# Reordering VectorE's work inside each phase of a fused state-space mixer, and moving three accumulator merges from GpSimd to VectorE

## The chip, the cores and the metric

The kernel runs on one core of one Trainium2 chip. The metric is the device time of one execution in microseconds (us); the time given for a kernel is the median of its runs. The five engines of the core are written as the profile writes them: PE (TensorE, matrix products), DVE (VectorE), ACT (ScalarE), POOL (GpSimd), SP (the queue that issues nearly all DMAs). PEld is PE's loading of weights, which runs beside its products.

## The reference

The input is 2 sequences of 512 tokens with 512 features, so 1024 tokens in 8 tiles of 128. Four residual blocks follow each other: a block-sparse linear layer, a quantised feed-forward block, a state-space mixer, and the feed-forward block again. The change touches only the mixer:

```python
proj = hidden_states @ in_proj_w.T               # gate | x, B, C | dt
xc = conv_general_dilated(xc, conv_w, ...) + conv_b   # causal, 4 taps, per channel
hBC = silu(transpose(xc))                        # x: 128 heads x 64; B, C: 8 groups x 128
dt = softplus(dt + dt_bias);  A = -exp(A_log)
Gm = einsum('bclhn,bcshn->bclsh', Cch, Bch)      # chunks of 128 tokens
M = Gm * exp(segment_sum(A * dt))                # decayed scores
Y_diag = einsum('bclsh,bcshp->bclhp', M, x * dt)
states = einsum('bclhn,bclhp->bchpn', B_decay, x * dt)   # carried from chunk to chunk
Y_off = einsum('bclhn,bchpn->bclhp', Cch, states) * state_decay
y = Y_diag + Y_off + D * x
y = y * rsqrt(mean(y**2) + eps) * norm_w * silu(gate)
return y @ out_proj_w.T
```

## The kernel before

**Phases.** The 8192 channels of x are 64 tiles of 128. A phase (`ph` 1 to 31) takes two of them, for both sequences: four *units*, `(0,0), (0,1), (1,0), (1,1)`. A phase overlaps three generations of work. For its own two tiles it computes the x projection (`x_front`), the convolution and the gate projection (`g_front`). For the tiles of the phase before it does the recurrence: transposed tokens (`tokens`), chunk states (`both_states`), decayed scores (`half_scores`, `back_scores`), the scan (`half_scan`) and the gating. For the tiles two phases back it does the output projection (`o()`, from `out_seven`). Phases 2 to 30 (`mid` in the code) have one written order of these steps. Phases 3, 7, 11, 15, 19, 23 and 27 also start the next group's B and C (`new_group`), and the phases 4, 8, ..., 28 after them compute that group's products of B and C (`group_scores`). Phase 31 is `final`: it does the output projection by plain products (`outs`).

**Order.** PE, ACT and DVE run in exactly the order in which the program is written (`manual_schedule`). POOL and SP are ordered by the scheduler. An instruction that waits holds up everything behind it on its engine.

**Seven-product blocks.** `seven` multiplies a 2x2 block matrix by Strassen's scheme in seven products over three PSUM banks x, y, z; `out_seven` does the same for two halves of the output projection, 14 products in a phase. In `seven` the third write of bank y may start only when DVE has read the second out of it: the product `s3*t3` (PE line 185) waits for the sum on line 206, the product `a22*t4` for that on line 211. In `out_seven` (PE line 1020, DVE sums on line 1034) the product 14 waits for DVE's sum of product 12, which reads the same bank.

**Deferred lists.** Two kinds of DVE work are kept in lists and issued when the program calls for them. `flush()` issues the waiting score products `m = m * gm` (line 900), which make the operands of the scan's products (line 919). `drain(3)` issues three convolution taps (line 734) of one 128x512 tile. `skipped` (line 939) takes the scan's result out of PSUM; `gated[k]()` (line 942) multiplies it with norm weight and gate. After that ACT squares y (line 948) and POOL adds the square to `sq_acc` (line 949).

**States.** `both_states(k)` multiplies into a PSUM bank (line 848). The first chunk's state is then copied, by ACT (line 857) where `by_act` is true and by DVE (line 859) otherwise, and the later chunks are formed by DVE, four instructions a unit (line 862).

**Merge.** In the output projection one product belongs to all four quarters of the accumulator `acc`. It is summed in a tile of its own, `common[0]`, and at the end of phase 30 `merge()` (line 1058) adds it to the other three quarters, with three 128x1024 additions on POOL.

Of the kernel before, what the change touches and what calls it, by code (L numbers as in the profile page):

```python
# [37 lines left out]
def kernel(  # L38
# [25 lines left out]
    nc = tc.nc  # L64
# [604 lines left out]
    def mixer(waiting, step_args, loaded):  # L669

        with ExitStack() as st:
# [18 lines left out]
            acc = x_sb  # L690
# [50 lines left out]
            def drain(n=None):  # L741

                n = len(taps) if n is None else min(n, len(taps))
                for f in taps[:n]:
                    f()
                del taps[:n]

            def silu(dst, src):
                nc.scalar.activation(dst, src, AF.Silu)  # L749

            def run(steps):
                for _ in steps:
                    pass
# [30 lines left out]
            n_ph = NCT // PP  # L784
# [26 lines left out]
            def g_front(left, gts, tags="proj"):  # L811

                for j, b in units:
                    gts[j, b] = act.tile([P, SEQ], F32, tag=f"gt{j}{b}", name="gt")
                later = []
                steps = seven(
                    left, tags, lambda j, b: gts[j, b], lambda j, b, ps: later.append((gts[j, b], ps)), False
                )
                return steps, later

            def x_tokens(ct, b, xc):

                h0 = 2 * ct
                cs = slice(b * NCH, (b + 1) * NCH)
                px = psum.tile([P, NCH, 2, HD], F32, tag="tr", name="x_tr")
                for c in range(NCH):
                    nc.tensor.transpose(  # L827
                        px[:, c].rearrange("p h d -> p (h d)"), xc[:, c * P : (c + 1) * P], ident
                    )
                x_dt = wrk.tile([P, NCH, 2, HD], F32, name="x_dt", bufs=4)  # L830
                nc.vector.tensor_tensor(
                    x_dt, px, dt[:, cs, h0 : h0 + 2].unsqueeze(3).to_broadcast([P, NCH, 2, HD]), ALU.mult
                )
                x_dec = wrk.tile([P, NCH - 1, 2, HD], F32, name="x_dec", bufs=2)
                nc.gpsimd.tensor_tensor(
                    x_dec,
                    x_dt[:, : NCH - 1],
                    dec[:, b, :, h0 : h0 + 2].unsqueeze(3).to_broadcast([P, NCH - 1, 2, HD]),
                    ALU.mult,
                )  # L840
                return x_dt, x_dec

            def states(ct, b, x_dec, b_tok, by_act):

                h0 = 2 * ct
                pst = psum.tile([P, NCH - 1, 2, HD], F32, tag="tr", name="pst")
                for c in range(NCH - 1):
                    nc.tensor.matmul(  # L848
                        pst[:, c].rearrange("p h d -> p (h d)"),
                        lhsT=b_tok[:, c, :],  # L850
                        rhs=x_dec[:, c].rearrange("p h d -> p (h d)"),
                        start=True,
                        stop=True,
                    )
                state = wrk.tile([P, NCH - 1, 2, HD], F32, name="state", bufs=4)
                if by_act:
                    nc.scalar.copy(state[:, 0], pst[:, 0])  # L857
                else:
                    nc.vector.tensor_copy(state[:, 0], pst[:, 0])
                for c in range(1, NCH - 1):  # L860
                    for hh in range(2):
                        nc.vector.scalar_tensor_tensor(  # L862
                            state[:, c, hh, :],
                            state[:, c - 1, hh, :],
                            e_last[:, b, c - 1, h0 + hh : h0 + hh + 1],
                            pst[:, c, hh, :],
                            ALU.mult,
                            ALU.add,
                        )
                return state  # L870
# [7 lines left out]
            def flush():  # L878
                for f in mults:
                    f()  # L880
                mults.clear()
# [65 lines left out]
            def squares(b, y):  # L947
                nc.scalar.activation(y, y, AF.Square)  # L948
                nc.gpsimd.tensor_add(sq_acc[:, b, :], sq_acc[:, b, :], y)  # L949

            def out_project(ph, ts, gts, wo, tag="yo", adds=None):
# [27 lines left out]
            common = []  # L979
            quarter = [  # L980
                (slice(b * NCH, (b + 1) * NCH), slice(n * DH, (n + 1) * DH)) for b in range(2) for n in range(2)
            ]
# [69 lines left out]
                        )  # L1052
                return steps

            def merge():

                for rows, cols in quarter[1:]:
                    nc.gpsimd.tensor_add(acc[:, rows, cols], acc[:, rows, cols], common[0])

            xcs, gts = {}, {}  # L1060
            groups = {}
# [2 lines left out]
            def half_scores(k, c, heads, later=None):  # L1064

                j, b = units[k // 2]
                if k % 2 == 0:
                    heads[j, b] = []
                    heads["bc"] = load_sums(c + j, b)
                heads[j, b].append(scores(c + j, b, k % 2, heads["bc"], later))  # L1070
# [44 lines left out]
            gate, later = g_front(wg, gts)  # L1115
# [40 lines left out]
            for ph in range(1, n_ph + 1):  # L1156
                front, last = ph < n_ph, ph >= 2
# [18 lines left out]
                def all_squares():  # L1176
                    for b, y in ys:
                        squares(b, y)
                    ys.clear()

                def tokens(k):
                    j, b = units[k]
                    xts[j, b] = x_tokens(c1 + j, b, xcs[j, b])

                def both_states(k, by_act=False):
                    for j, b in units[2 * k : 2 * k + 2]:
                        sts[j, b] = states(c1 + j, b, xts[j, b][1], groups[c1 // CTG][b][1], by_act)

                def back_scores(k):
                    half_scores(k, c1, heads)  # L1190
# [25 lines left out]
                if mid:  # L1216
                    outs7 = out_seven(lefts, rights, ph == 2)

                    def o():
                        product, summed = outs7.pop(0)  # L1220
                        product()
                        summed()

                    next(steps)
                    tokens(2)
                    tokens(3)
                    o()
                    next(steps)
                    back_scores(2)
                    o()  # L1230
                    o()
                    next(steps)
                    both_states(0, True)
                    back_scores(3)
                    o()
                    next(steps)
                    o()
                    flush()
                    next(steps)
                    drain(3)  # L1240
                    o()
# [9 lines left out]
                    gated = [f for _, f in scans]  # L1251
# [2 lines left out]
                    flush()  # L1254
                    back_scores(5)
                    o()
                    gated[0]()
                    o()
                    o()
                    flush()  # L1260
                    back_scores(6)
                    if made:
                        group_scores(made, groups[c0 // CTG], [0])
                    o()
                    gated[1]()
                    flush()
                    back_scores(7)
                    if made:
                        group_scores(made, groups[c0 // CTG], [1])
                    o()  # L1270
                    all_squares()
                    made = None
                    if ph == n_ph - 2:
                        merge()
                    if new_group:

                        flush()
                        steps, made = group((c0 + PP) // CTG, wbc, "yo")
                        for i, _ in enumerate(steps):
                            if i in (0, 1, 3, 5):  # L1280
                                drain(3)
                        gate, later = g_front(wg, gts_new)
                    else:
                        gate, later = g_front(wg, gts_new, ("proj", "yo", "yo"))
                        next(gate)
                        flush()
                    wx = load_pair(NCT + c0 + PP, NCT + c0 + PP + 1)
                    wo = load_out(ph - 1)
                    finish(half_scan(units[2:], "tr"))
# [11 lines left out]
                    for u in units:  # L1301
                        silu(xcs_new[u], xcs_new[u])
                    flush()
                    run(gate)
                else:
                    next(steps)
                    if not last:
                        group_scores(made, groups[0], [0])
                    else:
                        flush()  # L1310
                    next(steps)
                    if not last:
                        group_scores(made, groups[0], [1])
# [3 lines left out]
                        back_scores(2)  # L1317
                    tokens(2)
                    tokens(3)
                    next(steps)  # L1320
                    if last:
                        back_scores(3)
                    next(steps)
                    flush()
# [12 lines left out]
                    if not last:  # L1337
                        drain()
                        both_states(1)
                        gate, later = g_front(wg, gts_new)  # L1340
# [31 lines left out]
                    else:  # L1372
                        gate, later = g_front(wg, gts_new)
# [252 lines left out]
```

## Time and profile before

| | |
|---|---|
| median of 3 runs | 2304.89 us (2302.44 to 2306.73) |
| the profiled execution: its own time, its span | 2304.02 us, 2302.3 us |
| PE busy | 2242.4 us, 97% |
| DVE busy | 1805.7 us, 78% |
| POOL busy | 1243.9 us, 54% |
| ACT busy | 1180.2 us, 51% |
| mean granted PE clock | 0.998 |

The time is told by the span plus some 1.7 us around it (2304.02 less 2302.3). A busy PE is not a PE at its peak, so the 97% says only that PE is seldom without an instruction, not that the products are cheap. The stages stand in the timeline as follows: block-sparse layer and first feed-forward block up to about 330 us, mixer up to about 2035 us, second feed-forward block to the end. Within the mixer a phase of the plain kind is 49.2 us long (for instance from 622.73 to 671.96 us), one with a new group 62.4 us (671.96 to 734.32), the one after it 51.3 us (734.32 to 785.59).

### The profile page before, as it was taken

Reading aid. Unit: us, or ns where it says so; the run is one execution under the profiler, and the core shown is the slowest. Engines: PE = TensorE matmul, PEld = TensorE weight load, DVE = VectorE, ACT = ScalarE, POOL = GpSimd, SP = SyncE. Lnnn points to the kernel's source line nnn. Section 1 sums busy time; section 2 is a strip of 40 time slices with the busy share of each in tenths; the row PEclk is TensorE's granted clock in tenths of the full one; section 3 lists DMA queues with packets and bytes.
Section 4 is the critical chain, followed back from the end, with each engine's and each line's share of the span. In section 5 each row is a group of like instructions: output and inputs, shape, how many; then the busy total and the mean of one; then the engine's idle time right before and its main releaser. Section 6 shows DMA issues by size and latency. Waiting matters only on the chain.

```text
span 2302.3 us, 30183 instructions
## 1 busy us (share of the span) xinstructions
PE 2242.4 (97%) x10704; PEld 1411.4 (61%) x10704; DVE 1805.7 (78%) x3042; ACT 1180.2 (51%) x2532; POOL 1243.9 (54%) x1206
## 2 busy tenths in 40 slices
PE   9999999999999999999999999999999999999999
PEld 5445865656665666666566656666666665544468
DVE  5456568888888888888888888888888888865553
ACT  4111056756666665666566656656655666631100
POOL 3765024656655666566556555664665665527620
PEclk9999999999999999999999999999999999999999
DMA  5563021222222222222221222221222322326600
GB/s 188 191 199 105 28 74 55 74 74 65 73 74 65 74 85 71 74 74 74 64 74 65 77 68 75 74 83 58 81 75 63 110 65 74 119 83 223 201 24 28
DMA packets 145783, 201.59 MB, mean 88 GB/s; under 512 B 7136, under 2 KB 92000, under 8 KB 145632
## 3 DMA queue, kind: packets, MB, share of 16 engines
q1 hardware_dynamic: 145056, 198.61, 27.1%
q8 instruction: 85, 1.39, 0.3%
q10 hardware_dynamic: 576, 1.05, 0.1%
q14 instruction: 66, 0.54, 0.1%
HBM read 194.91 MB, written 4.72 MB: 87 GB/s over the span
## 4 chain that ended last, share of the span: by engine, by line
PE 83%; DVE 14%; issue 2%; ACT 1%; DMA 1%; POOL 0%; ACTq 0%; SPq 0%; POOLq 0%; DVEq 0%
PE proj L185 29%; PE yo L185 17%; PE po L1020 10%; PE ffn_o L556 7%; DVE m L900 5%; DVE x_sb L1034 5%; PE py L919 4%; PE pst L848 4%; PE py L928 3%; PE x_tr L827 2%; PE po L956 2%; DVE gt L942 1%; PE pg L486 1%; PE pu L486 1%; DVE xc L734 1%
## 5 line engine op out<-in xcount | busy, mean ns | idle before, releaser
L906 POOL TENSOR_TENSOR ce<-ce,c_t 128x384 f32<-128x384 f32 x256 | 267.7, 1051 | 340.7 <-ACT ce L902 335.0
L185 PE MATMUL proj<-xn_t,w 128*128 128x512 f32 x824 | 384.6, 593 | 2.0 <-DVE gt L206 1.7
L892 ACT ACTIVATE m<-bc,acs 128x128 f32<-128x128 f32 x1024 | 324.9, 390 | 4.4 <-PE py L919 4.4
L185 PEld LDWEIGHTS proj<-xn_t,w 128*128 128x128 f32 x824 | 153.0, 190 | 146.4 <-issue 137.7
L1034 DVE TENSOR_TENSOR x_sb<-x_sb,po 128x512 f32<-128x512 f32 x340 | 228.9, 679 | 9.5 <-PE po L1020 4.9
L171 POOL TENSOR_TENSOR ws<-w 128x256 f32<-128x256 f32 x96 | 72.9, 760 | 292.2 <-DMA w<-in_win_t_dram 242.1
L734 DVE SCALAR_TENSOR_TENSOR xc<-proj,cw,xc 128x511 f32<-128x511 f32 (+2 forms) x288 | 214.6, 746 | 6.6
L900 DVE TENSOR_TENSOR m<-m,gm 128x512 f32<-128x512 f32 x256 | 218.6, 876 | 0.0
L919 PE MATMUL py<-m,x_dt 128*64 128x128 f32 x2048 | 194.1, 278 | 13.7 <-DVE m L900 13.6
L949 POOL TENSOR_TENSOR sq_acc<-sq_acc,y 128x512 f32<-128x512 f32 x128 | 178.4, 1400 | 46.5 <-ACT y L948 43.8
L185 PE MATMUL proj<-tq,ws 128*128 128x512 f32 x432 | 199.2, 592 | 0.0
L1020 PE MATMUL po<-wo,gt 128*128 128x256 f32 x696 | 177.0, 384 | 0.0
L919 PEld LDWEIGHTS py<-m,x_dt 128*64 128x64 f32 x2048 | 135.8, 137 | 49.0 <-issue 25.8
L899 ACT ACTIVATE m<-m 128x512 f32<-128x512 f32 x256 | 161.3, 630 | 7.4
L185 PE MATMUL yo<-xn_t,w 128*128 128x512 f32 x328 | 151.7, 595 | 12.8 <-DVE tmp L206 12.8
L928 PE MATMUL py<-ce,state 128*64 128x128 f32 x1536 | 157.6, 274 | 0.0
L862 DVE SCALAR_TENSOR_TENSOR state<-state,e_last,pst 128x64 f32<-128x64 f32 x512 | 107.0, 276 | 60.2 <-ACT state L857 57.7
L185 PE MATMUL yo<-tq,ws 128*128 128x512 f32 x336 | 153.4, 599 | 0.2 <-ACT acs L714 0.2
L1020 PEld LDWEIGHTS po<-wo,gt 128*128 128x128 f32 x696 | 125.5, 190 | 30.9 <-issue 7.1
L749 ACT ACTIVATE xc<-xc 128x512 f32<-128x512 f32 x128 | 72.5, 621 | 134.3 <-DVE xc L734 133.9
L731 ACT ACTIVATE xc<-proj,cb,cw 128x512 f32<-128x512 f32 x96 | 74.4, 778 | 129.5 <-DVE proj L225 76.6
L942 DVE SCALAR_TENSOR_TENSOR gt<-y,nw,gt 128x512 f32<-128x512 f32 x128 | 137.1, 1071 | 2.5
(228 smaller groups left out, 4559.5 us busy)
## 6 DMA issues: line engine op xcount, KB each, us to landing
bc<-acs_d SPq DMA_DIRECT2D x128, 512.0 KB, 3.8
w<-in_win_t_dram SPq DMA_DIRECT2D x64, 512.0 KB, 3.8
wo<-in_wo_t_dram SPq DMA_DIRECT2D x31, 512.0 KB, 5.0
wi<-in_down_w_dram SPq DMA_DIRECT2D x14, 512.0 KB, 4.0
zi<-in_down_z_dram SPq DMA_DIRECT2D x14, 512.0 KB, 4.8
sf<-in_down_s_dram SPq DMA_DIRECT2D x14, 512.0 KB, 4.2
wi<-in_gate_w_dram SPq DMA_DIRECT2D x13, 512.0 KB, 4.3
zi<-in_gate_z_dram SPq DMA_DIRECT2D x13, 512.0 KB, 5.2
```

The costliest lines, as they stand in the source:

```text
L185: nc.tensor.matmul(ps, lhsT=a[:, kc, :], rhs=b[:, kc, :], start=(start and kc == 0), stop=(stop and kc == KH - 1), skip_group_check=True,)
L556: nc.tensor.matmul(ps, lhsT=a[:, k, :], rhs=b(k), start=(start and k == 0), stop=(stop and k == KF - 1), skip_group_check=True,)
L734: nc.vector.scalar_tensor_tensor(dst[:, s:], ps[:, : SEQ - s], cw[:, t, 3 - s : 4 - s], dst[:, s:], ALU.mult, ALU.add)
L892: nc.scalar.activation(m[:, c, :], bc[:, hh, c * P : (c + 1) * P], AF.Relu, bias=acs[:, t, h : h + 1], scale=-1.0,)
L899: nc.scalar.activation(m, m, AF.Exp, scale=-1.0)
L900: mults.append(lambda: nc.vector.tensor_mul(m, m, shared[b][2]))
L906: nc.gpsimd.tensor_mul(ce, ce, c_t[:, P:].rearrange("p (c l) -> p c l", l=P))
L919: nc.tensor.matmul(py[hh * HD : (hh + 1) * HD, c * P : (c + 1) * P], lhsT=x_dt[:, c, hh, :], rhs=m[:, c, :], start=True, stop=(c == 0),)
L928: nc.tensor.matmul(py[hh * HD : (hh + 1) * HD, c * P : (c + 1) * P], lhsT=state[:, c - 1, hh, :], rhs=ce[:, c - 1, :], start=False, stop=True,
L949: nc.gpsimd.tensor_add(sq_acc[:, b, :], sq_acc[:, b, :], y)
L1020: nc.tensor.matmul(banks[k][:, c, :], lhsT=a[:, t], rhs=b, start=(start and c == 0), stop=stop, skip_group_check=True,)
L1034: nc.vector.tensor_add(q, q, banks[k])
```

## The change

It has five parts.

1. In phases 2 to 30 the score products of the second pair (`back_scores(2)` and `(3)`) are issued on DVE before the states of the first pair rather than three steps after them; ACT works out `back_scores(3)` before, not after, `both_states(0)`. A `flush()` is added at the head of the phase; the list is empty there except in phase 2.
2. `both_states(0)` no longer has ACT copy the first states: two ACT copies a phase become two DVE copies.
3. The gatings: `gated[0]` is issued two output sums later, `gated[1]` after all eight score products and after the output sums.
4. With a new group, each pair of taps left over from x moves one step later, behind the sums of B's and C's products; the last three taps move to the end of the gate projection.
5. The three merges leave POOL at the end of phase 30 and are issued on DVE in phase 31, at three places.

```diff
-            def merge():
-                for rows, cols in quarter[1:]:
-                    nc.gpsimd.tensor_add(acc[:, rows, cols], acc[:, rows, cols], common[0])
+            def merge(k):
+                rows, cols = quarter[k]
+                nc.vector.tensor_add(acc[:, rows, cols], acc[:, rows, cols], common[0])
...
                     tokens(2)
                     tokens(3)
+                    flush()
                     o()
                     next(steps)
                     back_scores(2)
                     o()
                     o()
+                    back_scores(3)
                     next(steps)
-                    both_states(0, True)
-                    back_scores(3)
+                    flush()
+                    both_states(0)
                     o()
                     next(steps)
                     o()
-                    flush()
                     next(steps)
                     drain(3)
...
                     back_scores(5)
                     o()
-                    gated[0]()
                     o()
                     o()
+                    gated[0]()
                     flush()
                     back_scores(6)
...
                     o()
-                    gated[1]()
                     flush()
                     back_scores(7)
...
                     o()
+                    flush()
+                    gated[1]()
                     all_squares()
                     made = None
-                    if ph == n_ph - 2:
-                        merge()
                     if new_group:
-                        flush()
                         steps, made = group((c0 + PP) // CTG, wbc, "yo")
                         for i, _ in enumerate(steps):
-                            if i in (0, 1, 3, 5):
+                            if i in (1, 3, 5):
                                 drain(3)
                         gate, later = g_front(wg, gts_new)
                     else:
                         gate, later = g_front(wg, gts_new, ("proj", "yo", "yo"))
                         next(gate)
-                        flush()
...
                     flush()
+                    next(gate)
+                    drain(3)
                     run(gate)
                 else:
                     next(steps)
                     if not last:
                         group_scores(made, groups[0], [0])
                     else:
-                        flush()
+                        merge(1)
...
                     tokens(2)
                     tokens(3)
+                    if last:
+                        merge(2)
                     next(steps)
                     if last:
+                        merge(3)
                         back_scores(3)
```

PE's own order is the same before and after. On ACT only the two copies a phase go and `back_scores(3)` moves ahead of where they were. POOL's scheduled order follows: the third score's `ce` product (line 906) now stands ahead of the third and fourth `x_dec` (line 835), and the weight sums of the output projection (lines 988 to 990) stand between the two additions to `sq_acc` instead of behind both. SP's order is unchanged.

## The prediction

> **What bounds the kernel now.** I read the page first, then PE's waits over phases 2 to 30, then the timeline of a plain phase (616.7 to 666 us), a new-group phase and phases 2, 30 and 31, engine by engine.
>
> ```profile
> PE 2242.4 (97%) x10704; PEld 1411.4 (61%) x10704; DVE 1805.7 (78%) x3042; ACT 1180.2 (51%) x2532; POOL 1243.9 (54%) x1206
> PE 83%; DVE 14%; issue 2%; ACT 1%; DMA 1%; POOL 0%; ACTq 0%; SPq 0%; POOLq 0%; DVEq 0%
> ```
>
> PE bounds it: it is without an instruction for 60 us of 2302. The change leaves PE's instructions and their order alone, so all that can be won is time in which PE waits (and slow clock after it). PE's waits between 440 and 1940 us:
>
> ```profile
> PE py L919 <- DVE m L900: 13.6, 21, 2.3
> PE po L1020 <- DVE x_sb L1034: 12.9, 21, 0.6
> PE yo L185 <- DVE tmp L206: 12.8, 7, 1.8
> PE pgm L778 <- DVE gm L779: 1.9, 7, 0.3
> ```
>
> All are for DVE: 41.2 us, the ceiling apart from clock. One of each in the timeline:
>
> ```profile
> 648.37 1.13 PE L1020 MATMUL po<-ws,gt 128*128 128x256 f32 x4 [0.62 <-DVE x_sb L1034]
> ...
> 653.67 0.54 PE L919 MATMUL py<-m,x_dt 128*64 128x128 f32 x5 [0.56 <-DVE m L900]
> ...
> 705.72 3.70 PE L185 MATMUL yo<-xn_t,w 128*128 128x512 f32 x8 [1.83 <-DVE tmp L206]
> ```
>
> And what DVE does in a plain phase:
>
> ```profile
> 627.18 1.62 DVE L862 SCALAR_TENSOR_TENSOR state<-state,e_last,pst 128x64 f32<-128x64 f32 x8 [1.99 <-ACT state L857]
> ...
> 632.06 1.29 DVE L900 TENSOR_TENSOR m<-m,gm 128x512 f32<-128x512 f32 x2
> ...
> 652.17 1.45 DVE L900 TENSOR_TENSOR m<-m,gm 128x512 f32<-128x512 f32 x1
> ```
>
> DVE waits at the head of a phase (0.95, 1.10, 0.17, 1.99 and 0.73 us up to 630 us), then works almost without a gap until the next phase's transposes. It is late only in the second half. The change moves work into the gap at the head and lets the sums and score products for which PE waits go ahead of gatings, which PE needs only in the next phase.
>
> **The change, part by part (plain phase, 13 of them: 5, 6, 9, 10, ... 29).** *Score products and states.* ACT ends the exponential of the third score at 623.6; without the state copies (0.27 each, behind a wait of 2.88 for PE) it goes straight on with the fourth: four biases 1.28 and an exponential 0.63, ready at 625.9. DVE, free at 625.2, issues both products at 625.2 and 625.9: 1.3 us uncovered by POOL, up to 2.75 beside it (the row at 1952.44 of phase 31), so done by 626.6 to 627.9. Then two copies (0.28) and eight state steps (1.62): done by 629 to 630.1, where before it was 628.8. Behind them stands the sum on line 211, due for PE's `a22*t4` at 633.4: it ends at 631.0. So the added wait on ACT's exponential costs nothing; its cover is these 2.4 us. On POOL, the two later `x_dec` move behind one more `ce` (1.0 us): they end near 629.4, and their product starts at 637.7.
> The taps at 633.26 then start at 632.5, since they wait for ACT, which begins the convolution (0.81) after line 212. That lead of 0.8 us is lost again by 644: DVE meets the scan's results and the first output sums as PE delivers them (PE's second output product ends 644.31, before and after).
>
> *Gatings.* From there: sum at 645.55, then with `gated[0]` gone from its place the next two sums follow PE: the second ends at 647.55, where it was 648.3, and PE's product 14 starts unhindered: 0.62 us gone. Then gating, products and sums as before. The last score product was done at 653.62; now one gating (1.08) and 0.75 us of lateness are out of its way, so about 652.1, and PE, itself 0.62 earlier, wants it at 652.5: 0.56 gone.
> What is late next is line 206 of the gate projection, behind `gated[1]` and both remaining scans' gatings. With before's durations DVE needs, from 647.55, the 10.8 us that it needed from 646.15 to 658.12 less the two sums: 658.33. PE, without its two waits (1.18), wants it at 657.7, so 0.7 would be given back: gain 0.48. But some of those durations are POOL's doing:
>
> ```profile
> 651.79 1.28 POOL L949 TENSOR_TENSOR sq_acc<-sq_acc,y 128x512 f32<-128x512 f32 x1 [1.29 <-ACT y L948]
> ```
>
> Beside this the product at 652.17 took 1.45, and the gating at 649.89, beside the other, 1.16; alone they take 0.68 and 0.75. The addition follows ACT's square of the gating, so it moves with the gating, past the last product. If that saves 0.7 and 0.4 and costs 0.4 at the sixth product, the gain is near all of 1.18. Bounds 0.48 and 1.18; I take 0.9, nearer to the freed durations, which the rows show. 13 x 0.9 = 11.7 us.
>
> *New group, 7 phases.* Waits there: 0.62 and 1.83. The 1.83 is line 206 behind three taps (2.31). Now it stands behind `gated[1]` instead, and behind ACT's copy of line 202, which stands on ACT behind the square of `gated[1]`: gating ends near 701.9, square 0.6, copy 0.57, sum ready 703.85; PE wants it at 703.3: 0.6 stays. Then PE runs to the gate projection. Its second sums (lines 211, 212) wait for PE until 721.1, and behind them stand 7.8 us of DVE work up to the first `x_dt` of the next phase (two sums 1.3, three taps 2.2, two products 1.2, the three moved taps 2.3, two sums 1.2, and a little): ready at 729.95, wanted by PE's second transposes at 728.9. So a new wait of 1.1 us, transposes for line 831. Gain 2.45 - 0.6 - 1.1 = 0.75; bounds 0.2 and 1.85 (if only one of the two new waits comes). 7 x 0.75 = 5.3 us.
>
> *Phases after a new group, 7.* Waits 0.51 (scores) and 0.27 (`gm`). ACT is later here (it first does four more activations), the fourth score comes 1.3 us later against PE, and `gm` stands behind `gated[0]`: I keep about half, 0.4; bounds 0 and 0.78. 2.8 us.
>
> *Phases 2 and 30, and the clock.* Here PE's wait is followed by products at half speed. The columns of this window row are the stretch, its length, busy time and count of PE, PEld, DVE, ACT and POOL, granted clock, DMA share and GB/s:
>
> ```profile
> 426.00:434.00 8.00, 6.17 (x34) 4.76 (x31) 7.07 (x18) 6.96 (x19) 2.72 (x3) 0.79 0.20 66
> 1925.00:1932.00 7.00, 3.69 (x31) 3.15 (x30) 5.38 (x5) 5.68 (x12) 7.00 (x4) 0.76 0.23 72
> ```
>
> The Trainium skill, "TensorE: Matmul & The Clock Gate", section "Why this matters for your kernels", lets the clock fall only after idle gaps above about 3 us. By that rule nothing but the waits could be won. The trace shows it after 1.83 us (phase 2: eight products in 3.68 us, elsewhere 1.89) and after 0.97 and 2.33 (phase 30: 3.10 us to the end of the scan, elsewhere 1.68); I go by the trace, which adds 1.79 and 1.42 us. Phase 2: four score products in one block (2.49) made the scan's evacuation late; two of them move to a stretch where DVE sits 3.94 us, two to one of 1.80. Waits 1.83 + 0.27 + 0.53 and clock 1.79 make 4.4; I take 4.0, at least 2. Phase 30: the products beside POOL's merge took 2.85 and 2.24:
>
> ```profile
> 1923.12 2.85 DVE L900 TENSOR_TENSOR m<-m,gm 128x512 f32<-128x512 f32 x1
> 1926.49 2.24 DVE L900 TENSOR_TENSOR m<-m,gm 128x512 f32<-128x512 f32 x1
> ```
>
> Waits 0.61 + 0.97 + 2.33 and clock 1.42 make 5.3; less 0.3 at line 206, 5.0; at least 3.3.
>
> *Merges on DVE, phase 31.* No row shows them. The nearest is two 512-wide additions in one go, 1.28 us, so 3 x 1.28 = 3.8 us alone. The first fits the 2.30 us that DVE sits before line 206, the other two (2.56) just overfill the 2.35 before line 211. But POOL is busy from 1944.7 to 1955.9, and the two products at 1952.44 took 2.75 beside it, twice their time; "SBUF — State Buffer", section "Who interferes with whom", says a DVE instruction with two SBUF inputs waits for a whole reading GpSimd instruction. Alone, the merges would cost nothing. By rule and row the second one waits for POOL's square addition (to 1949.57) and ends at 1950.85, the third waits for the next POOL instruction (0.72) and ends at 1952.9: DVE is 1.8 us late at line 211. PE's `a22*t4` (1953.97) just allows that, but the lateness carries on to the evacuation of the scan (1964.9 for 1962.9), for whose bank PE's second `outs` product (1963.8) waits: 1.9 us. Bounds 0 and 4 (with slow clock); I take the 1.9.
>
> Sum: 11.7 + 5.3 + 2.8 + 4.0 + 5.0 - 1.9 = 26.9 us. 2302.3 - 26.9 = 2275.4 span; with the 1.7 around it 2277.1; the median of the runs lies 0.9 above the profiled execution (2304.89 against 2304.02), so 2278. The low ends together make a gain of 8.9 us, the high ends 43.5.
>
> **Rivals.** *A, DVE becomes the bound of the second half:* its work grows by 0.57 us a phase, and what PE no longer waits for at lines 919 and 1020 it waits for at line 206. For it: the unbroken DVE rows from 642 to 660. Against it: the freed POOL contention. Gain at the low ends, 9 to 15: 2290 to 2296. *B, all waits vanish:* no new wait at the transposes, none at line 206: 2261. For it: every wait is below the slack at the phase's head. Against it: the 7.8 us block behind the gate's sums. *C, slower:* the flush ahead of the states holds DVE for ACT's exponential, and states, output sums and line 211 queue behind it. It decides when DVE is later there than I reckon by the 2.4 us of cover plus the 0.9 us won in a phase, 3.3 us. Against it: even another table load on ACT (1.28) and POOL beside both products (1.5) make 2.8. If 4: 1.6 us x 29 - 27 = 19 slower, 2324. *D, the change does not take place:* DVE's order in the built program shows every move, so it gets nothing.
>
> **How the numbers follow.** Forecast 0.52; A 0.21; B 0.14; C 0.09; all gains eaten to within 0.2% 0.04. 0.2%, 4.6 us, is about what a measurement of this kernel can tell from no change. So faster 0.87, same 0.04, slower 0.09. The range, 2263 to 2294, leaves out the ends of A and B and all of C.
>
> **What would show it.** PE's wait for line 1034 gone; that for line 900 nearly gone; 7 waits at line 206 down from 1.8 to about 0.6; new ones of about 1 us at transposes for line 831, seven times; in phase 31 one near 2 us for line 939; the clock 1.0 in phases 2 and 30; plain phases of 48.3 us. Wrong: plain phases still 49.2, or PE waiting for lines 211 or 862.

## The result, and the profile after

The changed kernel takes 2297.93 us (median of 6 runs, 2295.32 to 2299.52) where the kernel before takes 2304.06 (6 runs, 2302.06 to 2306.73): a ratio of 0.9974, 95% interval 0.9963 to 0.9985. So it is faster, by 6.1 us, where 26.9 were forecast. The profiled execution of the changed kernel took 2297.72 us, its span is 2296.0.

The page's lines of busy time and of the chain that ended last:

```profile
PE 2248.0 (98%) x10704; PEld 1403.4 (61%) x10704; DVE 1850.8 (81%) x3103; ACT 1168.9 (51%) x2474; POOL 1277.3 (56%) x1203
...
PE 77%; DVE 20%; ACT 2%; issue 1%; DMA 1%; POOL 0%; ACTq 0%; SPq 0%; POOLq 0%; DVEq 0%
```

DVE is busy for 45 us longer (time in which it stands beside POOL counts as busy), and its share of the chain rose from 14% to 20%: more of the chain runs through it than before, not less. PE's waits from 440 to 1940 us (total, times, longest) say where:

```profile
PE x_tr L827 <- DVE x_dt L831: 14.6, 21, 1.2
PE yo L185 <- DVE tmp L206: 7.3, 7, 1.0
PE py L919 <- DVE m L900: 3.2, 15, 0.2
PE yo L185 <- DVE gt L206: 1.8, 8, 0.3
PE pgm L778 <- DVE gm L779: 1.6, 7, 0.2
```

The wait for line 1034 is gone, that for line 900 is down from 13.6 to 3.2 us. A new one is the largest: PE's second transposes wait for `x_dt` in 21 phases, where 7 were expected. Single rows of PE, one of each: in the second half of a plain phase; at the head of the new-group phase that follows it, where the wait is what the plain phase's end left behind; within that new-group phase; and at the head of the phase after it:

```profile
652.46 0.54 PE L919 MATMUL py<-m,x_dt 128*64 128x128 f32 x5 [0.21 <-DVE m L900]
...
667.99 1.23 PE L827 MATMUL x_tr<-ident,xc 128*128 128x128 f32 x8 [0.24 <-DVE x_dt L831]
...
704.22 3.70 PE L185 MATMUL yo<-xn_t,w 128*128 128x512 f32 x8 [1.04 <-DVE tmp L206]
...
730.58 1.25 PE L827 MATMUL x_tr<-ident,xc 128*128 128x128 f32 x8 [1.21 <-DVE x_dt L831]
```

The clock in the windows that were slow (phase 30 now ends 7.6 us earlier, so that the second window no longer covers the same products):

```profile
426.00:434.00 8.00, 6.92 (x74) 5.94 (x74) 7.86 (x20) 5.29 (x14) 3.89 (x5) 1.00 0.11 38
...
1925.00:1932.00 7.00, 7.00 (x17) 3.06 (x17) 6.35 (x10) 5.72 (x12) 2.82 (x3) 1.00 0.24 73
```

**By kind of phase.** PE's order is the same in both kernels, so a phase can be measured from its first transposes (`x_tr`, line 827) to the next phase's. Means in us; forecast and measured are the differences summed over the phases.

| phases | before | after | forecast | measured |
|---|---|---|---|---|
| plain (13) | 49.26 | 48.85 | -11.7 | -5.3 |
| new group (7) and the one after it (7) | 62.40 + 51.12 | 61.79 + 52.12 | -8.1 | +2.8 |
| 2 | 53.70 | 51.62 | -4.0 | -2.1 |
| 30 | 53.62 | 48.89 | -5.0 | -4.7 |
| 31 | 49.37 | 50.66 | +1.9 | +1.3 |
| sum | | | -26.9 | -8.0 |

The mixer's second phase began 1.7 us later in this execution (401.68 against 399.99); over all the traces below, whose programs are alike up to there, that moment scatters from 399.6 to 403.3. So -8.0 + 1.7 is the 6.3 us between the spans. 18.9 us of the forecast are missing, 17.3 of them in the plain phases and in the pairs around a new group. Of the 8.0 that came, some 3.2 are clock: before, the products after the waits in phases 2 and 30 ran at half speed (1.79 and 1.42 us, as the prediction read them), now they do not.

### The profile page after: what moved, and what is told of

Its sections match the earlier page's. It is cut to its first block, busy times and chain, and to the rows that moved or that the text cites. A ratio compares the mean times of both kernels' runs of the same rounds, so it can differ in the third digit from the quotient of the medians.

```text
span 2296.0 us, 30153 instructions
## 1 busy us (share of the span) xinstructions
PE 2248.0 (98%) x10704; PEld 1403.4 (61%) x10704; DVE 1850.8 (81%) x3103; ACT 1168.9 (51%) x2474; POOL 1277.3 (56%) x1203
## 4 chain that ended last, share of the span: by engine, by line
PE 77%; DVE 20%; ACT 2%; issue 1%; DMA 1%; POOL 0%; ACTq 0%; SPq 0%; POOLq 0%; DVEq 0%
PE proj L185 25%; PE po L1020 13%; PE yo L185 13%; PE ffn_o L556 7%; DVE m L900 5%; PE py L919 4%; PE pst L848 3%; DVE xc L734 3%; PE py L928 3%; DVE x_sb L1034 2%; DVE gt L942 2%; PE x_tr L827 2%; PE po L956 2%; PE pg L486 1%; PE pu L486 1%
## 5 line engine op out<-in xcount | busy, mean ns | idle before, releaser
L906 POOL TENSOR_TENSOR ce<-ce,c_t 128x384 f32<-128x384 f32 x256 | 299.5, 1174 | 343.0 <-ACT ce L902 337.2
L900 DVE TENSOR_TENSOR m<-m,gm 128x512 f32<-128x512 f32 x256 | 254.0, 1010 | 16.4 <-ACT m L899 16.4
L919 PE MATMUL py<-m,x_dt 128*64 128x128 f32 x2048 | 189.1, 277 | 3.3 <-DVE m L900 3.2
L919 PEld LDWEIGHTS py<-m,x_dt 128*64 128x64 f32 x2048 | 130.8, 137 | 36.8 <-issue 25.8
L948 ACT ACTIVATE y<-y 128x512 f32<-128x512 f32 x128 | 76.5, 622 | 140.5 <-DVE gt L942 140.5
L245 POOL TENSOR_TENSOR w<-w,sf 128x1024 f32<-128x1024 f32 (+1 forms) x30 | 70.0, 2335 | 111.8 <-DVE w L244 86.1
L902 ACT ACTIVATE ce<-bc 128x384 f32<-128x384 f32 x256 | 129.7, 507 | 0.0
L185 PEld LDWEIGHTS proj<-tq,ws 128*128 128x128 f32 x432 | 81.8, 190 | 76.7 <-issue 73.7
```

The source lines that it names most:

```text
L185: nc.tensor.matmul(ps, lhsT=a[:, kc, :], rhs=b[:, kc, :], start=(start and kc == 0), stop=(stop and kc == KH - 1), skip_group_check=True,)
L900: mults.append(lambda: nc.vector.tensor_mul(m, m, shared[b][2]))
L906: nc.gpsimd.tensor_mul(ce, ce, c_t[:, P:].rearrange("p (c l) -> p c l", l=P))
L919: nc.tensor.matmul(py[hh * HD : (hh + 1) * HD, c * P : (c + 1) * P], lhsT=x_dt[:, c, hh, :], rhs=m[:, c, :], start=True, stop=(c == 0),)
```

## The experiments

**What is late in a plain phase.** The end of a plain phase on DVE, before and after; with it POOL's rows of the same stretch. Before:

```profile
664.35 1.28 DVE L900 TENSOR_TENSOR m<-m,gm 128x512 f32<-128x512 f32 x2
...
663.10 1.27 POOL L1001 TENSOR_TENSOR sums<-gt,sums 128x512 f32<-128x512 f32 x1
```

After:

```profile
655.71 1.67 DVE L942 SCALAR_TENSOR_TENSOR gt<-y,nw,gt 128x512 f32<-128x512 f32 x1
...
663.66 2.39 DVE L900 TENSOR_TENSOR m<-m,gm 128x512 f32<-128x512 f32 x2
...
667.16 1.28 DVE L831 TENSOR_TENSOR x_dt<-x_tr,dt 128x512 f32<-128x512 f32 x2
...
655.57 1.26 POOL L949 TENSOR_TENSOR sq_acc<-sq_acc,y 128x512 f32<-128x512 f32 x1
...
662.81 1.27 POOL L1001 TENSOR_TENSOR sums<-gt,sums 128x512 f32<-128x512 f32 x1
664.04 1.46 POOL L906 TENSOR_TENSOR ce<-ce,c_t 128x384 f32<-128x384 f32 x1
```

The two score products begin 0.7 us sooner than before, and end later: 2.39 us for two instead of 1.28. POOL's last C factor (`ce`), 1.00 in other rows, takes 1.46 beside them. Before, POOL's last work ended at 664.37, just as the products began. Now `gated[1]` comes later, ACT's square and POOL's square addition come later with it (655.57), POOL's unbroken block is one instruction longer, and the scheduler has put one of its two `ce` behind the four sums of lines 998 to 1001, where both stood ahead of them before (from 656.81 us): this last `ce` reaches into the products. `x_dt` stands behind them, and PE's second transposes wait for it. The Trainium skill, "SBUF — State Buffer", section "Who interferes with whom", calls the port pair that both engines use an exclusive lock: whichever holds it, the other stands. Both rows stretch here, as that says, and by turns: taken singly, the first product ends at 664.63, 0.54 us after POOL's sum (664.09), POOL's `ce` at 665.50, and the second product at 666.05, 0.55 after that. Each side waited for the end of a whole instruction of the other.

That gave three theories: *collision* (the products are slow beside POOL), *load* (DVE has 0.57 us more to do in a phase, the copies), *order* (whatever stands ahead of `x_dt` is too much, alone or not). All runs but the last were executed once, so their times have no interval; the verdicts rest on the phase lengths, which for one kind of phase mostly repeat within 0.05 us, or else differ by steps of about 0.5 (more with the taps back, run 4). The changed kernel and the runs with the taps and with the merges back have the same program in their plain phases, and these average 48.81 to 48.91; in phase 2, also the same, they take 51.62, 52.21 and 52.20. So differences of the sum under some 2 us (an estimate from these) decide nothing. "Sum" runs from phase 2 to 31.

| kernel | us | sum | 2 | plain | new | after new | 30 | 31 |
|---|---|---|---|---|---|---|---|---|
| before | 2304.06 | 1591.7 | 53.70 | 49.26 | 62.40 | 51.12 | 53.62 | 49.37 |
| changed | 2297.93 | 1583.7 | 51.62 | 48.85 | 61.79 | 52.12 | 48.89 | 50.66 |
| C factors left out | 2285.95 | 1573.2 | 51.61 | 48.48 | 61.09 | 52.11 | 48.17 | 50.65 |
| copies back on ACT | 2296.30 | 1582.8 | 50.98 | 48.91 | 61.78 | 51.90 | 49.58 | 50.71 |
| gatings back | 2294.28 | 1582.9 | 53.38 | 48.99 | 60.18 | 53.10 | 48.99 | 50.65 |
| taps back | 2296.51 | 1585.2 | 52.21 | 48.81 | 63.64 | 50.41 | 49.42 | 50.65 |
| head's order back | 2299.02 | 1583.4 | 51.34 | 48.71 | 62.28 | 51.90 | 48.84 | 50.73 |
| merges back | 2301.27 | 1587.8 | 52.20 | 48.92 | 61.76 | 52.12 | 53.06 | 49.45 |
| first products at the head | 2280.35 | 1568.4 | 52.21 | 48.45 | 61.01 | 51.03 | 48.18 | 53.83 |
| mixed | 2268.68 | 1558.1 | 52.21 | 48.37 | 60.18 | 51.00 | 48.18 | 50.64 |

**1. C factors left out**: POOL's work beside the two products taken away.

```diff
                 if later is None:
-                    decayed()
+                    if heads is not skip_ce[0]:
+                        decayed()
```

`skip_ce[0]` is set only around the first two scores of the next phase, at the end of the phases 2 to 30; these lines are left out here.

> The changed kernel with the C factor of the first two scores of each phase from 3 on left out (POOL's products of line 906 that are issued at the end of the phases 2 to 30, two a phase), so the states' part of the output of those two steps is not scaled; DVE's, ACT's and PE's instructions and their order are untouched. Collision theory: nothing of POOL's lies beside DVE's two score products any more, which take about 1.3 us instead of 2.4; PE's wait at the second transposes goes from plain phases, which fall to about 48.6. Order and load theories: plain phases unchanged, about 49.0. After a new group, where POOL was done earlier, the wait of 1.2 us stays under every theory.

DVE and PE at the same place:

```profile
661.15 1.28 DVE L900 TENSOR_TENSOR m<-m,gm 128x512 f32<-128x512 f32 x2
...
665.08 1.04 PE L827 MATMUL x_tr<-ident,xc 128*128 128x128 f32 x8
```

Collision: the products take 1.28, the transposes wait for nothing, plain phases 0.37 shorter, and new-group phases, whose head has the same transposes, 0.70. The sum falls by 10.5 us: the collision cost that much, more than the change won. The phase after a new group stays where it was, so its wait has another cause.

**2. Copies back on ACT**, the load theory's own test.

```diff
-                    both_states(0)
+                    both_states(0, True)
```

> The changed kernel with the two state copies of the first pair back on ACT (0.27 each there, 0.28 on DVE). Load theory (DVE has 0.57 us more to do in a phase, and this is what makes it late at its end): plain phases 0.3 to 0.5 shorter, 48.4 to 48.6. Collision theory: the copies lie at the head, where DVE has slack, so plain phases stay at 48.7 to 49.0 (0 to 0.15 either way); ACT's fourth score waits behind the copies, as before, without effect on PE.

Plain phases 48.91 for 48.85, the two products 2.38 us: the load theory falls. (Phase 30 grew by 0.7, with 0.9 of wait at the same transposes. That is not the copies' doing: in the run with the taps back, whose phase 30 is the changed kernel's, it took 49.42 with the same wait.)

**3. Gatings back.**

```diff
                     o()
+                    gated[0]()
                     o()
                     o()
-                    gated[0]()
...
                     o()
+                    gated[1]()
                     flush()
                     back_scores(7)
...
                     flush()
-                    gated[1]()
                     all_squares()
```

> The changed kernel with the two gatings back in their old places (gated[0] behind the first output sum, gated[1] behind the third), everything else as changed. Collision theory: the 1.1 us a plain phase that did not come were lost because gated[1], moved back, takes ACT's square and POOL's square addition with it, so that POOL's last C factor (line 906, 1.46 us) runs into DVE's two score products at the end of the phase (2.39 us for two where 1.28 was usual). With the gatings back POOL is done before them: the two products take about 1.3, PE's wait at the second transposes for line 831 goes from the plain phases, while the waits for lines 1034 (0.6) and 900 (0.2 to 0.5) return; plain phases 48.9 to 49.2. Load theory (DVE simply has more to do, 0.57 us a phase for the state copies): the products are late anyway, waits at lines 1034, 900 and 831 all together, plain phases over 49.5. New-group phases about 61.0 (the wait behind the square and the copy of line 202 goes), the phases after them still 52.1.

DVE's products at the end of the plain phase, and POOL's C factors, now both done before them; then PE's waits from 440 to 1940 us:

```profile
663.88 1.28 DVE L900 TENSOR_TENSOR m<-m,gm 128x512 f32<-128x512 f32 x2
...
656.34 2.41 POOL L906 TENSOR_TENSOR ce<-ce,c_t 128x384 f32<-128x384 f32 x2
```

```profile
PE po L1020 <- DVE x_sb L1034: 11.2, 21, 0.5
PE py L919 <- DVE m L900: 9.3, 22, 0.6
PE x_tr L827 <- DVE x_dt L831: 8.5, 7, 1.2
...
```

As the collision theory had it: the wait at the transposes leaves the plain phases, those for lines 1034 and 900 return. It is the gatings' move that took the one wait away and brought the other; in sum the two kernels come out alike (1582.9 against 1583.7). The phases after a new group did not stay at 52.1 but grew to 53.10, since PE waits there for line 900 again (0.44 us, in the changed kernel none) and longer for line 779 (0.35 for 0.23): that part of the expectation missed. New-group phases fell by 1.6 us, more than expected. The reason, in the changed kernel on ACT and DVE:

```profile
702.34 0.63 ACT L948 ACTIVATE y<-y 128x512 f32<-128x512 f32 x1 [4.33 <-DVE gt L942]
702.87 0.57 ACT L202 COPY tmp<-yo 128x512 f32<-128x512 f32 x1
...
703.47 0.69 DVE L206 TENSOR_TENSOR tmp<-tmp,yo 128x512 f32<-128x512 f32 x1 [1.17 <-ACT tmp L202]
```

ACT sat 4.33 us waiting for `gated[1]` to square it, with the copy of line 202 queued behind the square, and PE's product waiting for the sum of that copy. With the gating back, DVE's sum starts at 702.05 and PE runs through.

**4. Taps back.**

```diff
-                            if i in (1, 3, 5):
+                            if i in (0, 1, 3, 5):
...
-                    next(gate)
-                    drain(3)
                     run(gate)
```

> The changed kernel with the last convolution taps of a new group back ahead of the gate projection's sum (line 206), everything else as changed. If the moved taps (2.31 us ahead of the first x_dt of the next phase) are the whole cause of the wait at the second transposes after a new group: that wait (1.2 us, seven times) goes, the phase after a new group falls from 52.12 to about 50.9, and the new-group phase rises from 61.6 to about 62.4 (wait at line 206 back at 1.8). The two together 113.2 to 113.7 us against 113.73 (changed) and 113.63 (before): so that moving the taps won nothing. If instead DVE's score products ahead of x_dt are what is late there, a wait of 0.3 to 0.6 stays in the phase after a new group, and it stays above 51.3. Plain phases as in the changed kernel.

The wait at the transposes after a new group goes (50.41) and the one at line 206 returns (2.0 us, seven times; 63.64, where about 62.4 was expected). Together 114.05 against 113.91. But in three of the seven new-group phases, those of 64.25 to 64.97 us, the products behind that wait run at half clock:

```profile
493.65 5.40 PE L185 MATMUL yo<-xn_t,w 128*128 128x512 f32 x8 [2.00 <-DVE tmp L206]
```

The other four average 63.00, with the phase after 113.4. So the taps' move carries a wait across the border of two phases and, clock apart, gained nothing: the pair is 0.5 us shorter here without it. What it saves is a wait so long that it can cost clock.

**5. The head's order back.**

```diff
                     tokens(3)
-                    flush()
                     o()
...
-                    back_scores(3)
                     next(steps)
-                    flush()
-                    both_states(0)
+                    both_states(0, True)
+                    back_scores(3)
                     o()
                     next(steps)
                     o()
+                    flush()
```

> The changed kernel with the head of each phase as before: no flush behind the tokens, states ahead of the fourth score with copies on ACT, the flush late. Gatings, taps and merges as changed. Four score products then stand in one place where two and two stood. If the head's order carried the gain of phase 2, that phase goes back from 51.6 to over 53; plain phases 49.1 to 49.3, since the run with the gatings back (48.99 against 49.26 before) leaves about 0.3 a phase for the head's order. If the head's order is worth nothing, plain phases stay at 48.85 and phase 2 at 51.6 to 52.2. Phase 30 tells the same as the run with the merges back: below 49.5 if the merges were its cause, over 51 if the states were.

The head's order brings nothing (sum 1583.4 against 1583.7). Plain phases fell to 48.71, new-group phases rose to 62.28: at 665.06 us the two products beside POOL take 3.16 us, and the transposes of the new-group phase wait 0.96 for `x_dt` (0.24 in the changed kernel). It is the same collision, met at another moment. And phase 2 did not go back; why is shown below, under Phase 2.

**6. Merges back on POOL**, at the end of phase 30.

> The changed kernel with the three merges of the accumulators back on POOL at the end of phase 30. If these are what made the two score products of phase 30 slow (2.85 and 2.24 us before, for 0.68), phase 30 goes back from 48.9 to 52.5 to 53.6 and phase 31 from 50.7 to 49.4: together 1.5 to 3.5 us slower than the changed kernel. If it was the order of states and score products that freed phase 30, it stays below 50 and the run is about 1.3 us faster than the changed kernel. All other phases unchanged.

POOL and DVE in phase 30 of this kernel, then PE:

```profile
1918.30 2.81 POOL L1058 TENSOR_TENSOR x_sb<-x_sb,w 128x1024 f32<-128x1024 f32 x1
...
1919.41 2.25 DVE L900 TENSOR_TENSOR m<-m,gm 128x512 f32<-128x512 f32 x1
...
1931.21 1.98 PE L185 MATMUL yo<-xn_t,w 128*128 128x512 f32 x4 [2.44 <-DVE gt L206]
```

Phase 30 goes back to 53.06, phase 31 to 49.45. So moving the merges won 4.2 us and cost 1.2, and with the old order of states, too, phase 30 is free (48.84, run 5): of all five parts it is the one that pays. (In this edit the `flush()` of phase 31 is back where `merge(1)` stood.)

**Phase 2.** The run with the head's order back has the four score products in one block again, and the wait of before nearly in full, yet phase 2 takes 51.34 us:

```profile
420.22 2.49 DVE L900 TENSOR_TENSOR m<-m,gm 128x512 f32<-128x512 f32 x4
...
433.08 1.99 PE L1020 MATMUL po<-ws,sums 128*128 128x256 f32 x8 [1.58 <-DVE y L939]
```

The eight products behind the wait run at full speed (1.99; before, after 1.83 us of waiting, 3.68). What phase 2 won is the clock, not the waits, and whether a wait of this length costs clock is in part chance (last section). In the changed kernel one of them even grew: PE's wait for POOL's `sums` (line 1000) went from 0.74 to 1.69 us, because the flush at the head puts two score products on DVE beside POOL's sums, and here it is POOL that is slowed (1.27 before). In the runs with the taps and the merges back, whose program is the same up to there, that wait is 1.19, and 0.78 and 0.77 are spent at line 211. In the changed kernel:

```profile
406.17 2.36 DVE L900 TENSOR_TENSOR m<-m,gm 128x512 f32<-128x512 f32 x2
...
406.19 1.79 POOL L999 TENSOR_TENSOR gt<-gt 128x512 f32<-128x512 f32 x1
407.94 1.72 POOL L1000 TENSOR_TENSOR sums<-sums,gt 128x512 f32<-128x512 f32 x1
```

**7. First products at the head.** If the products ahead of `x_dt` are the trouble, they can go behind it.

```diff
                     for u in units:
                         silu(xcs_new[u], xcs_new[u])
-                    flush()
                     next(gate)
```

> The changed kernel without the flush at the end of the phases 2 to 30: the first two score products of the next phase are then issued by the flush at its head, behind x_dt, instead of ahead of it. Collision and order theories: PE's wait at the second transposes for line 831 goes in every kind of phase; plain phases at most 48.6 (changed: about 49.0), phases after a new group about 51.0 (changed: 52.1). Load theory: DVE has the same work, so the lateness appears elsewhere at the head of the phase (line 900 or 862) and plain phases stay within 0.2 of the changed kernel's.

PE waits for `x_dt` nowhere between 440 and 1940 us. Plain phases 48.45, new-group phases 61.01, the phases after them 51.03: there it does not matter whether the products are slow (run 1 left that wait at 1.2), only that 1.28 us of them stand ahead of `x_dt`, with the three moved taps (taking these back removed the same wait, run 4). So *order* is right for these seven phases and *collision* for the rest. One phase lost: 31, whose head has another order, by 3.2 us, a wait with products at half clock behind it:

```profile
PE pst L848 <- DVE state L862: 2.8, 1, 2.8
```

**8. Mixed**: as run 7, but with the flush kept in phase 30, and the gatings of the new-group phases in their old places.

```diff
+                    if new_group:
+                        gated[0]()
                     o()
                     o()
-                    gated[0]()
+                    if not new_group:
+                        gated[0]()
...
+                    if new_group:
+                        gated[1]()
                     flush()
                     back_scores(7)
...
-                    gated[1]()
+                    if not new_group:
+                        gated[1]()
...
-                    flush()
+                    if ph == n_ph - 2:
+                        flush()
```

> The changed kernel with two edits: the flush at the end of the phases 2 to 29 is left out (the first two score products go to the flush at the next phase's head; at the end of phase 30 it stays), and in the seven phases with a new group, and only there, the gatings stand in their old places. Theory: what the change lost, it lost to the products ahead of x_dt (with POOL's C factor beside them) and, in a new group, to gated[1] and ACT's square ahead of the sum for the convolution's projection. Then: plain phases 48.2 to 48.7 (mean 48.45), new-group phases about 60.2 (no wait at line 206), the phases after them about 51.0, phase 31 about 50.7 again (53.8 without its flush). Sum against the run without the flush: 3.2 less in phase 31, 5.8 less in new groups; time about 2271 us, 0.986 of before. If the gatings in the new-group phase were only free because PE waited elsewhere, the new-group phases stay at 61.0 and the time at about 2277.

2268.68 us (5 runs, 2267.04 to 2270.85), 0.9851 of before, 95% interval 0.9838 to 0.9865; the phases are as expected, plain ones 0.08 shorter still. Its page and PE's waits from 440 to 1940 us:

```profile
PE 2237.3 (99%) x10704; PEld 1405.4 (62%) x10704; DVE 1849.2 (82%) x3103; ACT 1163.4 (51%) x2474; POOL 1297.1 (57%) x1203
...
PE 86%; DVE 10%; ACT 1%; issue 1%; DMA 1%; SPq 0%; POOL 0%; ACTq 0%; DVEq 0%
```

```profile
PE po L1020 <- DVE x_sb L1034: 3.7, 7, 0.5
PE py L919 <- DVE m L900: 3.1, 15, 0.2
PE pgm L778 <- DVE gm L779: 1.6, 7, 0.2
PE yo L185 <- DVE gt L206: 1.1, 5, 0.2
...
```

DVE's busy time is that of the changed kernel (1849.2 against 1850.8), PE's 41.2 us of waits before are some 10. The work was not too much; it stood in the wrong order.

## Why the prediction was wrong

*Right.* The ceiling and the method: PE's order is fixed, waits are all there is, and mixed wins 33.6 us in these phases, 3.2 of them clock. The wait for line 1034 is gone, that for line 900 nearly so, and it was the gatings that did it, as the prediction's second step said (run 3). Phase 30: 4.7 won for 5.0. The clock is 1.00 in phase 2. Line 206 of a new group waits for ACT's copy behind the square, 1.04 us where 0.6 was reckoned; the transposes after a new group wait 1.21 where 1.1 was. Rival C, the states held by ACT's exponential, did not occur: no wait for line 862 appears in the changed kernel's list. (The other sign of being wrong, PE waiting for line 211, did come in phase 2, 0.78 us, in the runs with the taps and the merges back.) In plain phases the copies cost nothing (run 2), as said.

*The step that failed first: "gain near all of 1.18; I take 0.9".* Measured: 0.41. It followed the square addition one step, past the last score product, counted what is freed there, and stopped at line 206. The addition landed on the last gating ahead of line 206 (655.71: 1.67 us, before 1.09). And POOL's block does not end there. Its last `ce` runs into two more DVE products at the end of the phase, where 1.28 us became 2.39, with `x_dt` and PE's transposes behind. Run 1 prices it: 0.37 us in a plain phase and 0.70 in a new-group phase on average, 0.72 in phase 30; 10.5 in sum. That turned the forecast's 48.3 us for a plain phase into 48.85; without the collision it is 48.48. The rest is line 206 (the low bound's "given back"): in mixed, phases with that wait of 0.22 us take 48.65 to 48.69, those without it 48.18.

*The pair around a new group: "gain 0.75" and "I keep about half, 0.4".* Measured +0.40 instead of -1.15. 0.70 of this 1.55 is the collision, which meets PE at the head of the new-group phase; the forecast counted it nowhere. 0.44 is line 206, 0.11 the transposes. The last 0.3 is not settled. In part it is how a wait is listed: it counts from the modelled end of the product before, and the first group after it runs longer too (eight transposes 1.25 instead of 1.04, eight products 3.70 instead of 3.60). From start to start the transposes of phase 8 cost 1.54 for a listed 1.21, and the wait that went at line 919 gave back 0.88 for 0.51; but two output products (line 1020) also began 0.23 later with no wait listed. The prediction added listed waits.

*Phase 2: "I take 4.0".* The clock part came (1.79), though the reason given for it, the length of the wait, does not hold (last section): that part is luck. The waits did not: 1.08 remained at line 939, and 0.95 was added at POOL's sums, which the prediction did not follow: it reckoned what POOL does to the moved products and not what they do to POOL. That spreading the four products was the cure is refuted by run 5.

*Phase 31: +1.9, measured +1.3, by another way.* The merges were as slow as reckoned:

```profile
1936.90 1.22 DVE L1058 TENSOR_TENSOR x_sb<-x_sb,w 128x1024 f32<-128x1024 f32 x1
...
1941.09 3.87 DVE L1058 TENSOR_TENSOR x_sb<-x_sb,w 128x1024 f32<-128x1024 f32 x2
...
1951.21 0.94 PE L848 MATMUL pst<-x_dec,b_tok 128*128 128x128 f32 x6 [0.34 <-POOL x_dec L835]
```

Alone 1.22 us each, the last two 1.94 each beside POOL. But the first wait on PE is for POOL's `x_dec`, queued on POOL behind what the merges had slowed, and not for line 939.

*The rivals.* A came nearest in time (2290 to 2296), with its reason half right: what PE no longer waits for at lines 919 and 1020 came back elsewhere, at the transposes, in plain and new-group phases through POOL, and not through the 0.57 us of load (run 2).

## What to carry to other kernels

When an instruction moves, follow the whole chain that it releases (here gating, ACT's square, POOL's addition, the end of POOL's block) to the next place where POOL and DVE would both work, and ask for each of the two what stands behind it. Work that nobody needs soon belongs behind the instruction for which the bottleneck waits, even by one place: one `flush()` left out was worth more than the whole change. Price each part by undoing it alone, phase by phase: four of the five parts moved waits about, and only the merges paid clearly as they stood.

## What the runs showed of the hardware

*The clock does not follow the length of the wait, but where the wait lies.* In the profile before, products ran at half speed after 1.83 us of waiting. In the run with the merges back PE waited 2.44 us, and the products after it show full clock. So neither the prediction's reading (a wait of that size costs clock) nor the 3 us of the Trainium skill, "TensorE: Matmul & The Clock Gate", section "Why this matters for your kernels", tells the two apart.

The traces kept of the ten kernels do. In them the half clock comes in stretches of 3.41 us (three times two in a row; the last one is cut by the end), and within a trace these begin whole multiples of 3.413 us apart: before, at 429.89, 1928.34 and 2030.74 us, which is 439 and 30 steps. So each trace can be cut on that grid. Two pieces of before, three of the merges back; the second number of a row, behind the length, is PE's busy time, and the clock stands third from the end:

```profile
426.48:429.89 3.41, 1.58 (x13) 0.96 (x9) 3.34 (x13) 2.91 (x8) 0.32 (x1) 1.00 0.00 0
429.89:433.30 3.41, 3.41 (x8) 2.72 (x9) 2.55 (x4) 3.38 (x11) 2.00 (x2) 0.50 0.46 154
```

```profile
1926.80:1930.22 3.42, 1.96 (x5) 0.57 (x3) 3.38 (x3) 3.39 (x10) 3.42 (x3) 1.00 0.00 0
1930.22:1933.63 3.41, 2.42 (x6) 1.23 (x7) 3.34 (x6) 3.35 (x6) 2.19 (x2) 1.00 0.13 52
1933.63:1937.04 3.41, 3.41 (x9) 1.50 (x9) 3.31 (x6) 0.13 (x2) 0.00 (x0) 1.00 0.28 107
```

The wait of 1.83 us lies whole in one piece, that of 2.44 is split over two. Over some 6500 pieces between 30 and 2255 us, all ten in which PE was busy for at most 1.41 us were followed by half clock. Of the seven with 1.58 to 1.60 us two were, and of those with more only one, itself a piece at half clock. In these traces, then, a piece in which PE stands for more than about half costs clock in the next one, some 1.7 us (an estimate: half of 3.41); a wait of 1.83 us reaches that border only if no grid line cuts it, and even then it may not (at 702.95 us of before, 1.57 us busy, the clock stayed). That is why phase 2 was partly chance. Where exactly the border lies stays open.

*The collision costs both sides, and its size depends on the moment,* since each waits for the end of the other's instruction. The same two products took 1.28 us alone, 2.39 in the changed kernel and 3.16 in the run with the head's order back; of POOL's additions of 1.27, one took 1.79 in phase 2 (line 999) and one 2.26 in phase 31 (line 949).
